# Layer 3's last FFN unit beside the attention's head, its second call in halves, and products of constants in layer 1

## The chip, the cores and the metric

The kernel runs on one core of a Trainium2 chip. A core has five engines with queues of their own: TensorE (PE) multiplies matrices into PSUM, VectorE (DVE), ScalarE (ACT) and GpSimd (POOL) work on what lies in SBUF or PSUM, and SyncE (SP) starts most transfers.[...] The metric is the device time of one launch in microseconds. The kernel before took 2889.82 us (median of three runs, 2889.73 to 2892.66).

## What is computed

Four sequences of 512 rows and 128 features pass through four layers. Each layer is a half-weighted FFN, an attention and the same FFN again:

```python
x = x + 0.5 * _L1_ffn_ref(_layernorm(x, axis=-1), ...)
x = x + _L1_attn_ref(_layernorm(x, axis=-1), ...)
x = x + 0.5 * _L1_ffn_ref(_layernorm(x, axis=-1), ...)
...
x = x + 0.5 * _L3_ffn_ref(_layernorm(x, axis=-1), ...)
x = x + _L3_attn_ref(_layernorm(x, axis=-1), ...)
x = x + 0.5 * _L3_ffn_ref(_layernorm(x, axis=-1), ...)
return x
```

Layer 1's "FFN" contains a causal attention of 16 heads of 8 features, followed by experts of which two are chosen per row. Layer 3's attention has the same heads without a mask. Layer 3's FFN is two transformer blocks with attention over windows of 64 rows; this is one block, without its attention:

```python
x = x + o @ wo
h = shift_token(x)
mu = h.mean(-1, keepdims=True)
var = h.var(-1, keepdims=True)
h = (h - mu) / jnp.sqrt(var + 1e-05) * lg + lb
h = h @ w1 + b1
a, g = jnp.split(h, 2, axis=-1)
h = a * jax.nn.gelu(g, approximate=False)
x = x + h @ w2 + b2
```

All values are float32. A float32 product appears in the trace as two instructions of PE.

## The kernel before

Everything stays in SBUF: x and its normed copy y with rows on partitions, yT with features on partitions. b counts the four sequences, S = 512 is the length of one, P = 128, TB = 4 tiles of 128 rows. The stages run in the order of the reference. Instructions marked "in order" (mm_in_order, L163, and the like) keep the program's order on their engine; the others are placed by a scheduler.

**Dense attention** (dense_attention, L735) serves layer 1's FFN, called twice (masked), and layer 3's attention (not masked). There are 16 units, one for each sequence b and each j of 0 to 3; a unit has four steps, a step two halves. A half of maxima (L751) multiplies queries and marked keys of two head groups, in products that use 32 rows of the array, into one of two "q" banks, and DVE takes the row maxima (L772 masked, L767 not). queries turns a unit's maxima (pm) and adds them to the queries (qx). scores multiplies again into the one "k" bank (pk), weights takes the exponential on ACT (L802), and with_values multiplies with the values into the one "o" bank (po). Maxima run LEAD = 5 steps ahead of scores, so the loop at L869 starts at step -5: these first ten halves of maxima, with what prepare does before them for b = 0 (normed features, queries, keys, values; its early steps are called at once, L863), are the **head**. In the last five steps, the **tail**, there are no maxima left. The PSUM banks are MIX: two banks as one "k" tile, two "q" tiles of two banks, one "o" and one "m". All other products share the single "m".

**Chains and ticks.** Work that isn't urgent is put into a chain: a list of small steps, each with a gap. tick (L259) is called after every half and runs the chain steps that are due, at most one with products. In this way a finished sequence is normed for the next stage (leave_normed: statistics, scaling, turn), and layer 1's experts are worked off. With routed set, in layer 1's second call, each sequence also gets its router logits.

**Layer 3's FFN** (l3_ffn, L1549) has eight units, one for each of two blocks and each b, with four steps each. project, to_features, weights, exponentials, turn_weights and with_values are the window attention, in a pipeline six steps deep. What follows in a unit is a list of parts (L1809), each with the step after which it comes: attended (pz, the output product, and the shifted copy h2), mean (pm), variance (pvar, and an inverse root in ten small steps on POOL, L1739), spread (dg), normed (pb), hidden three times (two products of 512 columns each, pag, then GELU and a multiplication, hh), close_unit (pz2) and leave (pt_z; adds to x, and in the first call norms it for the attention, in the second sends it out). For all but the last unit the parts lie among the next unit's steps. For the last unit, b = 3 of the second block, the loop at L1820 runs on for 14 steps with nothing beside the parts. Then l3_attn opens its own pools and begins with b = 0.

Of the kernel before, what the change touches and what calls it, by code (L numbers as in the profile page):

```python
# [28 lines left out]
P = 128  # L29
# [74 lines left out]
def tile_macaron(ctx, tc, x_in, const_in, vec_in, w0_in, ws_in, ws3_in, w2f_in, w3_in, out):  # L104
# [61 lines left out]
    def transpose_in_order(dst, src):  # L166
        tc.keep_in_program_order(transpose(dst, src))

# [566 lines left out]
    def dense_attention(sb, prepare, finish, wo, masked, tiles=None):  # L735
# [119 lines left out]
        for u, (b, j) in enumerate(units):  # L855
# [6 lines left out]
            if j == 0:  # L862
                for at, f in prepare(b, seq(b)["vh"], seq(b)):  # L863
                    if b or at >= -LEAD:
                        later.setdefault((n + math.floor(at), int(at % 1 * 2)), []).append(f)
                    else:
                        f()

        for n in range(-LEAD, n_steps + 5):  # L869
            for half in range(2):  # L870
                pk = scores(n, half) if 0 <= n < n_steps else None
                if n + LEAD < n_steps:
                    maxima(n + LEAD, 1 - half)
                if pk is not None:
                    weights(n, half, pk)
# [673 lines left out]
    def l3_ffn(w3, tag, first):  # L1549
        with pool(tag) as sb, banks(tag + "ps", d=3, m=2):  # L1550
# [8 lines left out]
            def tmp(name):  # L1559
                return sb.tile([P, S], F32, tag="tmp", name=name, bufs=4)  # L1560
# [7 lines left out]
            def pair(name):  # L1568
                return bank("d", name)

            def shift(dst, src):

                act_copy(dst[0:64], src[0:64])
                nc.gpsimd.memset(dst[64:128, 0:1], 0.0)
                nc.vector.tensor_copy(dst[64:128, 1:S], src[64:128, 0 : S - 1])
# [116 lines left out]
            def with_values(step):  # L1692
# [12 lines left out]
                if t == 0:  # L1705
                    u_state[u]["oT"] = sb.tile([P, 4, S], F32, tag="oT", name="oT")
# [3 lines left out]
            def attended(u):  # L1710
                l, b = units[u]
                oT = u_state[u]["oT"]
                pz = bank("m", "pz")
                for fc in range(4):
                    mm_in_order(pz, W(l, "wo").rearrange("p (c n) -> p c n", n=D)[:, fc, :], oT[:, fc, :], fc == 0, fc == 3)
                z = yT[:, b, :]
                nc.vector.tensor_add(z, pz, z)
                h2 = sb.tile([P, S], F32, tag="h2", name="h2", bufs=2)
                shift(h2, z)
                u_state[u]["h2"] = h2  # L1720

            def mean(u):
                h2 = u_state[u]["h2"]
                pm = bank("m", "pm")
                mm_in_order(pm, onesm, h2)
                nc.vector.tensor_sub(h2, h2, pm)
                sq = tmp("sq2")
                act(sq, h2, AF.Square)
                u_state[u]["sq"] = sq

            def variance(u):

                sq = u_state[u].pop("sq")
                pv = bank("m", "pvar")
                for t in range(TB):
                    mm_in_order(pv[:, 2 * t : 2 * t + 2], sq[:, ts(t, P)], onesm[:, 0:2])
                rs = sb.tile([P, TB], F32, tag="rs", name="rs", bufs=2)
                nc.vector.tensor_copy(rs, pv[:, : 2 * TB].rearrange("p (t i) -> p t i", i=2)[:, :, 0])
                inverse_root(sb, rs, rs, "ir4", ALU.add, 1e-5, nc.gpsimd)  # L1739
                u_state[u]["rs"] = rs  # L1740

            def spread(u):

                rs = u_state[u].pop("rs")
                dg = tmp("dg")
                nc.vector.scalar_tensor_tensor(
                    dg.rearrange("p (t n) -> p t n", n=P), rows(ident, TB), float(D), bcast(rs, P), ALU.mult, ALU.mult
                )
                u_state[u]["dg"] = dg

            def normed(u):
                l, b = units[u]
                h2 = u_state[u]["h2"]
                pb = bank("m", "pb3")
                mm_in_order(pb, onesm, u_state[u].pop("dg"))
                nc.vector.scalar_tensor_tensor(h2, h2, W(l, "lg"), pb, ALU.mult, ALU.mult)

            def hidden(u, c):
                l, b = units[u]
                at, n = HCH[c]  # L1760
                h2, w1 = u_state[u]["h2"], W(l, "w1")
                if c == 0:
                    u_state[u]["hh"] = sb.tile([P, 3, S], F32, tag="hh", name="hh")
                p = pair("pag")
                mm_in_order(p[:n, 0:512], w1[:, HID + at : HID + at + n], h2)
                mm_in_order(p[:n, 512:1024], w1[:, at : at + n], h2)
                ge = tmp("ge")
                act(ge[:n, :], p[:n, 0:512], AF.Gelu, bias=W(l, "b1g")[:n, c : c + 1])
                nc.vector.scalar_tensor_tensor(
                    u_state[u]["hh"][:n, c, :], p[:n, 512:1024], W(l, "b1a")[:n, c : c + 1], ge[:n, :], ALU.add, ALU.mult  # L1770
                )

            def close_unit(u):
                l, b = units[u]
                hh = u_state[u]["hh"]
                w2 = W(l, "w2").rearrange("p (c n) -> p c n", n=D)
                z = yT[:, b, :]
                pz = bank("m", "pz2")
                for c, (_, n) in enumerate(HCH):
                    mm_in_order(pz, w2[:n, c, :], hh[:n, c, :], c == 0, c == 2)  # L1780
                nc.vector.scalar_tensor_tensor(z, pz, W(l, "b2"), z, ALU.add, ALU.add)
                del u_state[u]

            def leave(b):
                pt = bank("m", "pt_z")
                for t in range(TB):
                    transpose_in_order(pt[:, ts(t, P)], yT[:, b, ts(t, P)])
                xb = x[:, ts(b, TB), :].rearrange("p t d -> p (t d)")
                nc.vector.scalar_tensor_tensor(xb, pt, 0.5, xb, ALU.mult, ALU.add)
# [218 lines left out]
```

## Time and profile before

| | before |
|---|---|
| median of the runs | 2889.82 us |
| profiled execution | 2886.26 us |
| span of its trace, first to last instruction | 2884.6 us |
| granted TensorE clock, mean | 0.871 |
| PE busy | 2245.8 us (78%) |
| DVE busy | 1788.8 us (62%) |
| ACT busy | 1243.1 us (43%) |
| POOL busy | 911.9 us (32%) |

A profile is one execution. The view in 40 slices gives each engine's busy share in tenths and, as PEclk, the clock that the throttle granted TensorE. A matmul takes longer at a lower clock and still counts as busy, so a busy PE with a low clock is a slow one. The timeline gives start, duration, engine, line, operation, and in brackets how long the engine had been idle and what ended that.

### The profile page before, as it was taken

The page shows a single profiled execution, that of the slowest core. Times are in us where ns is not written, and L with a number is a line of the kernel's source. Part 1 is how long each engine was busy: PE and PEld are TensorE (multiplying, and loading weights), DVE is VectorE, ACT ScalarE, POOL GpSimd, SP SyncE. Part 2 cuts the span into 40 slices and gives each one's busy share as a digit, 9 for nine tenths or more (in the row PEclk, how much of TensorE's full clock was granted, in tenths as well). Part 3 has the DMA queues.
Part 4 walks back from the last instruction along what each step waited for, and adds up shares of the span by engine and source line. Part 5 has one row for each costly group of instructions (what it writes and reads, how often), then busy time and mean ns, then how long its engine had stood idle before and what let it go on. Part 6 is the DMA issues. An engine that isn't in the chain of part 4 may idle for free. (4 is left out here: it accounts for less than half of the span.)

```text
span 2884.6 us, 46981 instructions
## 1 busy us (share of the span) xinstructions
PE 2245.8 (78%) x17562; PEld 1171.8 (41%) x17562; DVE 1788.8 (62%) x4844; ACT 1243.1 (43%) x2678; POOL 911.9 (32%) x1704
## 2 busy tenths in 40 slices
PE   4387448988678899758668578997789998789987
PEld 2154123333343333347458455555322222455553
DVE  4745576775675677544754577776356554777763
ACT  3154214433333433313423277776134444567763
POOL 1022012233121231213313486774100000777661
PEclk8578659999887999869868799999689999899998
DMA  3052010000000000027007210000000000110000
GB/s 135 11 158 67 0 59 1 1 1 1 1 1 1 1 1 5 4 75 257 9 16 272 72 25 19 22 21 8 0 1 1 1 1 1 26 23 21 22 20 12
DMA packets 33772, 99.14 MB, mean 34 GB/s; under 512 B 6184, under 2 KB 12072, under 8 KB 33032
## 3 DMA queue, kind: packets, MB, share of 16 engines
q1 hardware_dynamic: 30616, 88.03, 9.4%
q0 software_dynamic: 2496, 5.12, 0.8%
q8 instruction: 139, 2.28, 0.3%
q10 hardware_dynamic: 432, 2.98, 0.3%
q14 instruction: 89, 0.73, 0.1%
HBM read 66.88 MB, written 14.55 MB: 28 GB/s over the span
## 5 line engine op out<-in xcount | busy, mean ns | idle before, releaser
L802 ACT ACTIVATE PT<-pk_at 128x1024 f32<-128x1024 f32 (+3 forms) x384 | 310.8, 809 | 543.9 <-PE pq_at L164 470.6
L164 PE MATMUL pk_at<-qx,km 32*128 32x512 f32 (+3 forms) x1536 | 368.1, 556 | 61.3 <-ACT PT L802 56.3
L164 PE MATMUL po_at<-PT,vh 128*32 128x512 f32 (+3 forms) x1536 | 328.7, 510 | 4.4 <-POOL PT L805 4.2
L772 DVE CUSTOM_DVE_ANT_0 s<-pq_at,cst 128x384 f32<-128x384 f32 (+3 forms) x512 | 248.4, 485 | 97.2 <-PE pq_at L164 85.8
L1563 ACT ACTIVATE s<-s,nm,rn 128x128 f32<-128x128 f32 x512 | 245.5, 482 | 2.1 <-DVE nm L1669 1.9
L805 POOL TENSOR_SCALAR_AFFINE_SELECT PT<-PT 128x256 f32<-128x256 f32 x256 | 106.8, 419 | 411.5 <-ACT PT L802 411.4
L164 PE MATMUL pq_at<-km,qT 32*128 32x384 f32 (+3 forms) x1024 | 225.2, 528 | 13.7 <-DVE nm L772 7.3
L164 PEld LDWEIGHTS pk_at<-qx,km 32*128 32x128 f32 x1536 | 119.7, 189 | 266.2 <-ACT PT L802 206.7
L767 DVE TENSOR_REDUCE nm<-pq_at 128x2 f32<-128x1024 f32 x128 | 156.2, 1225 | 104.4 <-PE pq_at L164 103.9
L1618 POOL TENSOR_TENSOR t<-t,t 128x1024 f32<-128x1024 f32 x64 | 151.3, 2364 | 132.1 <-DVE t L1614 131.7
L161 PE MATMUL pt_y<-ident,y 128*128 128x128 f32 x224 | 55.1, 376 | 157.6 <-DVE y L214 118.4
L164 PE MATMUL p_qk<-w,hT 128*128 128x512 f32 x256 | 146.5, 701 | 11.0 <-DVE t L1614 9.1
L164 PE MATMUL pq_at<-km,t 32*128 32x512 f32 x512 | 149.4, 689 | 7.0 <-DVE nm L767 4.9
L164 PEld LDWEIGHTS po_at<-PT,vh 128*32 128x32 f32 x1536 | 55.7, 109 | 222.2 <-issue 144.0
L161 PE MATMUL pt<-ident,s 128*128 128x128 f32 x640 | 92.2, 291 | 62.8 <-POOL s L1681 36.7
L241 ACT COPY yT<-pt_y 128x512 f32<-128x512 f32 x56 | 32.7, 584 | 242.8 <-PE pt_y L161 242.7
L1681 POOL TENSOR_TENSOR s<-s,sm 128x1024 f32<-128x1024 f32 x64 | 121.4, 1897 | 49.3 <-DVE sm L1680 41.2
L1611 DVE TENSOR_TENSOR t<-p_qk,w 128x1024 f32<-128x1024 f32 x64 | 78.3, 1223 | 71.7 <-ACT sq L1563 71.4
L1563 ACT ACTIVATE sq<-p_qk 128x1024 f32<-128x1024 f32 x64 | 65.5, 1023 | 127.7 <-PE p_qk L164 76.0
L161 PEld LDWEIGHTS pt<-ident,s 128*128 128x128 f32 x640 | 77.5, 149 | 95.2 <-POOL s L1681 51.5
L161 PEld LDWEIGHTS pt_y<-ident,y 128*128 128x128 f32 x224 | 35.0, 173 | 188.3 <-issue 119.0
L1305 DVE SCALAR_TENSOR_TENSOR hT<-pa,w,sg 128x128 f32<-128x128 f32 x184 | 51.8, 344 | 84.8 <-ACT sg L1304 63.7
(428 smaller groups left out, 5145.3 us busy)
## 6 DMA issues: line engine op xcount, KB each, us to landing
w<-in_w2f_dram SPq DMA_DIRECT2D x46, 836.0 KB, 5.9
vb<-v SPq DMA_DIRECT2D x112, 128.0 KB, 2.2
skew<-qe SPq DMA_DIRECT2D x16, 512.0 KB, 3.0
rel<-skew SPq DMA_DIRECT2D x64, 128.0 KB, 3.3
w<-in_w_dram SPq DMA_DIRECT2D x1, 4147.0 KB, 12.4
w<-in_w_dram SPq DMA_DIRECT2D x1, 3200.0 KB
od<-o SPq DMA_DIRECT2D x46, 64.0 KB, 5.0
yd<-y SPq DMA_DIRECT2D x8, 256.0 KB, 2.3
```

The costliest lines, as they stand in the source:

```text
L161: return nc.tensor.transpose(dst, src, ident[: src.shape[0], : src.shape[0]])
L164: tc.keep_in_program_order(nc.tensor.matmul(dst, lhsT=lhsT, rhs=rhs, start=start, stop=stop))
L241: by_order(nc.scalar.copy(yT[:, b, :], pt))
L767: nc.vector.tensor_reduce(to, pq.rearrange("p (i n) -> p i n", i=2), AX.X, ALU.max)
L772: nc.vector.tensor_tensor_reduce(s[:, :nk], pq[:, i * 512 : i * 512 + nk], causal[:, S - nk :], 1.0, -BIG, ALU.add, ALU.max, nm[:, qt, at ...
L802: by_order(nc.scalar.activation(PT[:, :, q0:], pk[:, :, q0:], AF.Exp, scale=SC8))
L805: nc.gpsimd.affine_select(d, d, pattern=[[0, 2], [1, P]], base=0, channel_multiplier=-1, compare_op=ALU.is_ge, fill=0.0)
L1305: nc.vector.scalar_tensor_tensor(hT[s][:, c, :], pa[:, ts(c, P)], b1[:, c : c + 1], sg, ALU.add, ALU.mult)
L1563: tc.keep_in_program_order(nc.scalar.activation(*args, **kw))
L1611: nc.vector.tensor_mul(by_head(t1), by_head(p3), over(tab[:, 0]))
L1618: nc.gpsimd.tensor_add(t1, t1, t2)
L1681: nc.gpsimd.tensor_mul(s, s, bcast(sm, P))
```

## The change

Layer 1's dense attention gets products of two constants (onesm, a matrix of 1/128, and columns of the constants cst) into a PSUM bank that nobody reads: of 512 columns after each step of the head that prepare calls at once, of 256 in each half of the head's loop, and in the second call of 256 in each half of the tail. Layer 3's attention, which isn't masked, gets a tick in place of the first kind.

The last unit of layer 3's FFN leaves the list of parts. In the first call its steps become a chain, so that the ticks of the attention's head run them, one at a time, with the attention's PSUM banks; leave of the unit before stands among them. Its tiles come from a pool that outlives both stages. In the second call each step is done in two halves of 256 columns, and the unit before leaves after the first step. The last unit's inverse root is on DVE in both calls.

```diff
@@ -166,6 +166,10 @@
     def transpose_in_order(dst, src):
         tc.keep_in_program_order(transpose(dst, src))
 
+    def idle_product(tag, n):
+
+        mm_in_order(bank(tag, "idle")[:, :n], onesm, cst[:, :n])
+
     def bcast(ap, n):
 
         return ap[:, :, None].to_broadcast([ap.shape[0], ap.shape[1], n])
@@ -865,12 +869,20 @@
                         later.setdefault((n + math.floor(at), int(at % 1 * 2)), []).append(f)
                     else:
                         f()
+                        if masked:
+                            idle_product("o", S)
+                        else:
+                            tick()
 
         for n in range(-LEAD, n_steps + 5):
             for half in range(2):
                 pk = scores(n, half) if 0 <= n < n_steps else None
                 if n + LEAD < n_steps:
                     maxima(n + LEAD, 1 - half)
+                if masked and n < 0:
+                    idle_product("o", S // 2)
+                elif masked and routed and n_steps - LEAD <= n < n_steps:
+                    idle_product("q", S // 2)
                 if pk is not None:
                     weights(n, half, pk)
                 if 1 <= n <= n_steps:
...
-    def l3_ffn(w3, tag, first):
+    def l3_ffn(w3, tag, first, rb):
...
-                return bank("d", name)
...
+                return bank("d" if "d" in psum["bufs"] else "q", name)
+
+            def shift(dst, src, at=slice(0, S)):
+
+                act_copy(dst[0:64, at], src[0:64, at])
+                a = max(at.start, 1)
+                if at.start == 0:
+                    nc.gpsimd.memset(dst[64:128, 0:1], 0.0)
+                nc.vector.tensor_copy(dst[64:128, a : at.stop], src[64:128, a - 1 : at.stop - 1])
...
+            def attended(u, at=whole):
                 l, b = units[u]
                 oT = u_state[u]["oT"]
+                n = at.stop - at.start
                 pz = bank("m", "pz")
                 for fc in range(4):
-                    mm_in_order(pz, W(l, "wo").rearrange("p (c n) -> p c n", n=D)[:, fc, :], oT[:, fc, :], fc == 0, fc == 3)
+                    mm_in_order(
+                        pz[:, :n], W(l, "wo").rearrange("p (c n) -> p c n", n=D)[:, fc, :], oT[:, fc, at], fc == 0, fc == 3
+                    )
                 z = yT[:, b, :]
...
+                nc.vector.tensor_add(z[:, at], pz[:, :n], z[:, at])
+                if at.start == 0:
+                    u_state[u]["h2"] = rb.tile([P, S], F32, tag="h2", name="h2", bufs=2)
+                shift(u_state[u]["h2"], z, at)
...
+                eng = nc.vector if u == len(units) - 1 else nc.gpsimd
+                inverse_root(rb, rs[:, :n], rs[:, :n], f"ir{n}", ALU.add, 1e-5, eng)
...
+            def hidden(u, c, at=whole):
...
+                mm_in_order(p[:n, 0:m], w1[:, HID + a : HID + a + n], h2)
+                mm_in_order(p[:n, 512 : 512 + m], w1[:, a : a + n], h2)
...
+            def leave(b, at=whole):
                 pt = bank("m", "pt_z")
+                t0, n = at.start // P, (at.stop - at.start) // P
+                for t in range(n):
+                    transpose_in_order(pt[:, ts(t, P)], yT[:, b, ts(t0 + t, P)])
+                tiles = slice(b * TB + t0, b * TB + t0 + n)
...
-                    nc.sync.dma_start(out[:, ts(b, TB), :], x[:, ts(b, TB), :])
+                    nc.sync.dma_start(out[:, tiles, :], x[:, tiles, :])
...
-            later = {}
+            later, last = {}, len(units) - 1
             for u in range(len(units)):
-                for f, after, place in parts:
+                for f, after, place in parts[: -1 if u == last - 1 else None] if u < last else ():
                     later.setdefault((u * TB + after, place), []).append((f, u))
...
+            rest = [attended, mean, variance, spread, normed]
+            rest += [lambda u, at, c=c: hidden(u, c, at) for c in range(3)] + [close_unit, lambda u, at: leave(units[u][1], at)]
+            if first:
+                spare = chain(units[last][1])
+                for f in rest:
+                    spare(1, lambda f=f: f(last, whole), f is not spread)
+                    if f is variance:
+                        spare(1, lambda: leave(units[last - 1][1]))
+            else:
+                for f in rest:
+                    for at in (slice(0, S // 2), slice(S // 2, S)):
+                        f(last, at)
+                    if f is attended:
+                        leave(units[last - 1][1])
 
 
...
-    l3_ffn(w3, "l3f", True)
-    l3_attn()
-    l3_ffn(w3, "l3g", False)
+    with pool("l3r") as rb:
+        l3_ffn(w3, "l3f", True, rb)
+        l3_attn()
+        l3_ffn(w3, "l3g", False, rb)
```

mean, variance, spread, normed, hidden and close_unit take the same argument at as attended, and work on its columns. In the order of instructions that the change gives, layer 1's first call has two idle products ahead of its first turn, the second call three ahead of pw; the first of each waits for DVE's last reader of the bank. One scaling of layer 3's tables by vec stands behind the keys of the first head instead of ahead of them. In layer 3's attention PE's order is pz, p of the keys, pm, p, pvar, pt_z of b = 2, p of the queries, p, pb, and then products of maxima with the three pag pairs, pz2, pt_z and pt_y between them.

## The prediction

> **What bounds the kernel now.** I began with the page's 40 slices, because the change names three places, and looked for idle TensorE and for a low granted clock there.
>
> ```profile
> span 2884.6 us, 46981 instructions
> ...
> PE   4387448988678899758668578997789998789987
> ```
>
> That line must be read with the clock line of the same view; one slice is 72 us.
>
> ```profile
> PEclk8578659999887999869868799999689999899998
> ```
>
> The clock is half in the slice at 361 to 433 us (layer 1's first dense attention begins at 388; the other 5 is layer 0, not touched) and low again in those at 1154 and 2019 us. A slice hides shorter dips, so around the changed places I cut the trace into stretches of 4 or 5 us: busy microseconds and instructions of PE, weight loads, DVE, ACT, POOL, then the granted clock.
>
> ```profile
> 416.00:420.00 4.00, 3.62 (x15) 1.72 (x13) 3.00 (x14) 0.00 (x0) 0.00 (x0) 0.50 0.00 0
> 420.00:424.00 4.00, 3.95 (x17) 1.79 (x17) 1.99 (x10) 0.17 (x1) 0.00 (x0) 0.50 0.00 0
> 900.00:904.00 4.00, 2.71 (x12) 0.52 (x8) 1.49 (x5) 1.18 (x2) 0.41 (x1) 0.50 0.00 2
> 1190.00:1195.00 5.00, 5.00 (x14) 0.88 (x12) 0.00 (x0) 1.62 (x2) 0.57 (x2) 0.50 0.00 0
> 2098.00:2102.00 4.00, 4.00 (x12) 1.65 (x12) 2.96 (x3) 0.00 (x0) 0.00 (x0) 0.50 0.00 0
> 2118.00:2122.00 4.00, 3.81 (x21) 0.90 (x18) 2.43 (x2) 2.05 (x2) 0.00 (x0) 1.00 0.00 0
> ```
>
> TensorE is busy yet at half speed, so in these heads (and in the tail at 1190) it is the bound through its clock. The timeline gives the price of half speed for one shape, the four instructions of a half's score products:
>
> ```profile
> 1165.32 1.13 PE L164 MATMUL pk_at<-qx,km 32*128 32x512 f32 x4
> 1166.44 2.08 PE L164 MATMUL pq_at<-km,qT 32*128 32x512 f32 x4
> ```
>
> Layer 3 is bound otherwise, by chains in which one engine works and the rest wait. Last FFN unit of the first call, first product of the attention, its first exponential:
>
> ```profile
> 2033.72 3.70 PE L164 MATMUL pz<-oT,w 128*128 128x512 f32 x8 [0.21 <-DVE oT L1707]
> ...
> 2070.53 2.07 PE L164 MATMUL p<-yT,ws 128*128 128x512 f32 x2 [0.68 <-ACT yT L241]
> ...
> 2106.97 1.02 ACT L802 ACTIVATE PT<-pk_at 128x1024 f32<-128x1024 f32 x1
> ```
>
> So 36.8 us of FFN remainder and then 36.4 us of attention head, one after the other; only b=3 is in the first, only b=0 in the second. The end of the kernel is the same remainder:
>
> ```profile
> 2852.97 3.70 PE L164 MATMUL pz<-oT,w 128*128 128x512 f32 x8 [0.21 <-DVE oT L1707]
> ...
> 2864.84 0.69 DVE L1746 SCALAR_TENSOR_TENSOR dg<-ident,rs 128x512 f32<-128x512 f32 x1 [2.85 <-POOL rs L194]
> ...
> 2868.58 7.64 PE L164 MATMUL pag<-h,w 128*128 128x512 f32 x12 [0.92 <-DVE h L1756]
> ...
> 2880.50 0.69 DVE L1789 SCALAR_TENSOR_TENSOR x<-pt_z,x 128x512 f32<-128x512 f32 x1 [0.75 <-PE pt_z L161]
> ```
>
> 28.2 us from pz to the last x, and 3.4 us more to the end of the span.
>
> **Part 1, idle products.** Added: 12 products of 512 columns and 30 of 256, full 128 rows. Such a product of 512 takes 0.86 us at full clock (p_qk: four instructions in 1.72 us on the chain that ended last) and 2.08 us at half (pk at 402.39); of 256, half of each by length. They add 23 us of PE time at full clock, all in heads and one tail.
>
> Here a rule speaks against the part. The Trainium skill (TensorE: Matmul & The Clock Gate, Part 1) says that some 3.4 us of sustained matmuls release the throttle. By it a busy stream warms itself, the idle products only add work, and the part costs a few us. The rows above disagree: PE busy 5.00 of 5 us at 1190, and 4.00 of 4 at 2098, at clock 0.50. What these share is products of 32 rows, two at a time, half the array. Full-row streams do rise: the pag products from 2868.58 run at 1.04 us each and from about 2872.4 at 0.43, after 3.8 us. I go by the rows: full rows between the half-filled ones should raise the clock and hold it.
>
> First call. PE runs on from pt_y at 392.0, so I put the rise at about 396. The first two idle products wait for DVE's last reader of that bank (x<-pb, to 386.4); only pt_y at 392.0 is behind them. The one after pt_y delays pw by about 1 us; then pq and pk take 0.9 instead of 2.08, and km comes at 401.8 instead of 405.1. One scaling of w by vec (1.18 us, DVE) now stands behind km, where it was hidden before: maxima begin at 403.9 instead of 406.6, gain 2.6. From there to qx is 14.4 us now. DVE's own work in it is 9.9 us (4 x 0.74 at 512, 4 x 0.60, 4 x 0.47, 6 x 0.33, values 0.69); PE with an idle product needs 0.86+0.43 at 512, less than DVE's 1.48. So about 10.5: gain 3.9. The first two steps cost 3.2 and 2.65 instead of 2.3: gain 1.2. **7.5 us.**
>
> Second call. Three idle products stand ahead of pw, after the linear attention's last reader (874.3): pw 2.6 us later. pq and pk at full clock give back most; km is 0.4 later. The maxima to qx take 10.5 instead of 14.0 (883.8 to 897.8), and the steps from 898.5 to 911.2, 12.7 us at half clock, take 8.3 by the pace at full clock (2.3 each at 512, from 918.2 to 920.5; 1.85 each at 384, from 427.6 to 431.2). 3.5+4.4-0.4 = **7.5 us**.
>
> Tail. From 1186.2 to 1201.8 ten halves alternate pk and po at half clock. At full clock with an idle product they take some 11 us (PE-bound: 0.65+0.43+0.86 at 384). Of 4.5 I keep **3 us**, since DVE's expert sums follow at 1202.5 and the gate's chain on DVE ends only at 1188.4.
>
> These operations were not in the trace; the bounds for the three together are 24 us gained and, if all stay at half clock, 44 lost (below).
>
> **Part 2, the remainder beside the head.** Nothing is removed but b=3's place: its steps go one per tick between those of attention b=0. They share the attention's single "m" bank, so each product waits for the reader of the one before. I walked PE's and DVE's new order with the rows' durations (1.13 a product with its latency, 0.7 a DVE pass of 512, POOL's add 1.26, maxima 1.23). pz 2033.7 to 2037.4; yT 38.1; p(k), pm, p(ks), pvar, pt_z of b=2, p(q), p(qs), pb, each some 1.9 us apart with its reader: pb ends at 2053.5. The inverse root is on DVE (8 x 0.2), interleaved. Ahead of the first maxima DVE has h and the four scalings of b=2 (1.1), so these begin at 55.8. Then ten halves of maxima with three pag pairs, pz, pt_z and pt_y between them, DVE-bound at about 2 us: qx at 75.5, exponential at 77.2. Against 2106.97 that is 29.8. But around 2043 to 2050 PE does little but pvar and transposes, and before, the clock fell about 1 us after just such a pvar (it ends at 2861.8; the row of 2860 to 2864 shows 0.86, so 2.9 us of it at 1.00). If it falls, three products and the first pag lose some 6 us before it rises. I take **24 us**; bounds 14 (all at half clock: six products +0.95, three pag +1.9, ten halves with little cover) and 30. Behind the moved steps: b=3's statistics and scalings (2.7 us of DVE) now lie among maxima, hidden by PE's pace of 2.3 a half, else +1. POOL's four memsets (2.4 us) and the bias adds to x wait for nobody on the path; POOL loses ten root steps. SP gets nothing here.
>
> **Part 3, the end in halves.** pz0 ends at 54.8, pz1 at 56.7; while one half is on PE the other is on DVE or ACT. A DVE pass of 256 costs 0.42 against 0.69 (maxima at 256), so split passes cost DVE 0.15 each. x of b=2 now stands before h of the second half (0.7). sub 59.5, sq 60.0, pvar 60.6, both roots on DVE to 62.1 and 63.2 (POOL took 62.07 to 64.80 for one), pb, first h at 64.0 where it was 68.5: gain 4.5. pag: 12 x 0.43 = 5.2 at full clock, 7.5 if it has fallen as before (7.64). From its end to x 3.8 instead of 5.0, for hh, pz2, yT, pt_z and x are each half as long. Gain 5.9 with a fallen clock, 8.1 without. **6.5 us.** SP issues two output transfers of half size; only the second counts, and the 3.4 us stay.
>
> **Sum.** 7.5+7.5+3+24+6.5 = 48.5 us. The profiled execution took 2886.26 us (span 2884.6 and 1.7 around it), which gives 2837.8; the median of the runs shown is 3.6 above it: **2841**.
>
> **Rivals.**
> - *The idle products raise the clock but don't hold it*; part 1 is worth nothing net: -30.5, 2859. For it: the second head reached 0.76 in the row of 888 to 892 and fell to 0.50. Against it: no full-row product stood between the maxima there.
> - *Layer 3's head stays cold*: 14 instead of 24, and the end at 5: 2851. For it: at 2070 to 2082 PE was busy two thirds with full-row products at 0.50. Against: it starts from full clock this time.
> - *Slower*: idle products don't count for the clock. Place: the two heads and the tail. At half clock each of 256 costs 1.04 on a bound PE: 30 x 1.04 = 31; those of 512 put 4 us into the first chain and 9 into the second: 44 in all. It decides once that passes the 30 which layer 3 gives: 2904. Only the pag row speaks against it, and strongly.
> - *The change doesn't do what it says*: layer 3's one bank keeps the two chains in series. The new order shows p(k) directly behind pz, so I give it little.
>
> **How the numbers follow.** Forecast 0.60 (own range 2828 to 2852), no hold 0.17, cold head 0.15, slower 0.05, in series 0.03 (about no change). The lower end 2824 takes the upper bounds of all parts (24+30+8), the upper end 2866 covers both milder rivals together in part. A measurement of this kernel can tell about 0.2% (5.8 us) from no change: faster 0.92, same 0.03, slower 0.05.
>
> **What would show it.** Clock 1.0 from about 396 to 430 and from 874 to 915; first exponential of layer 3's attention some 43 us after pz; first h of the last unit 11 us after pz. Wrong if the rows at 400 to 424 keep 0.50, if the maxima of layer 3 wait for pag's bank more than for DVE, or if another stage changes by more than 5 us.

## The result and the profile after

| | us |
|---|---|
| before, median of 4 runs (lowest to highest) | 2891.24 (2889.73 to 2894.17) |
| changed, median of 4 runs (lowest to highest) | 2860.84 (2856.48 to 2867.22) |
| ratio, 95% interval | 0.9895 (0.9873 to 0.9917) |
| profiled execution before / changed | 2886.26 / 2856.48 |
| changed again, on another chip: median, ratio | 2855.85, 0.9871 (0.9853 to 0.9889) |

The change saves 30 to 37 us of 2890; the forecast was 48.5. From the view in 40 slices (now 71 us each) the two lines that were shown of before, TensorE's busy tenths and its granted clock:

```profile
span 2854.8 us, 47242 instructions
...
PE   4377468988678898859566678998799999688988
...
PEclk8588769999889998959777789999899999899998
```

The clock's digit went from 5 to 6 in the slice that begins at 357 us (first head), from 7 to 9 at 856 (second head), from 8 to 9 at 1142 (tail) and from 6 to 8 at 1998 (layer 3's head). But behind the tail, at 1213, it went from 6 to 5. The same cut into short stretches as before (busy microseconds and instructions of PE, weight loads, DVE, ACT, POOL, then the granted clock):

```profile
392.00:396.00 4.00, 4.00 (x6) 1.30 (x4) 4.00 (x11) 0.20 (x1) 2.09 (x2) 0.50 0.00 0
396.00:400.00 4.00, 3.84 (x8) 1.35 (x8) 3.51 (x11) 0.77 (x2) 0.00 (x0) 0.94 0.00 0
...
416.00:420.00 4.00, 2.40 (x20) 0.73 (x12) 2.35 (x7) 2.52 (x3) 1.62 (x2) 1.00 0.00 0
420.00:424.00 4.00, 3.96 (x20) 1.02 (x20) 1.58 (x6) 0.81 (x1) 0.81 (x2) 0.57 0.00 0
900.00:904.00 4.00, 2.81 (x20) 0.77 (x20) 2.51 (x9) 1.76 (x3) 0.81 (x2) 1.00 0.01 2
1190.00:1195.00 5.00, 5.00 (x28) 2.11 (x28) 0.55 (x2) 1.56 (x3) 0.81 (x2) 1.00 0.00 0
...
2098.00:2102.00 4.00, 3.68 (x24) 0.91 (x24) 1.89 (x3) 1.42 (x3) 0.00 (x0) 1.00 0.00 0
```

All the stretches that stood at 0.50 now show 1.00, except 420 to 424: the idle products do raise the clock, where the forecast put the rise (396), and hold it until they stop. Layer 3's head and the end of the kernel, from the timeline:

```profile
2038.71 3.67 PE L164 MATMUL pz<-oT,w 128*128 128x512 f32 x8 [0.89 <-DVE oT L1725]
...
2052.36 2.08 PE L164 MATMUL p<-yT,ws 128*128 128x512 f32 x2 [1.19 <-DVE x L1815]
...
2089.62 1.02 ACT L806 ACTIVATE PT<-pk_at 128x1024 f32<-128x1024 f32 x1 [5.73 <-PE pq_at L164]
...
2829.16 3.72 PE L164 MATMUL pz<-oT,w 128*128 128x256 f32 x16
2829.28 0.69 DVE L1725 COPY oT<-po 128x512 f32<-128x512 f32 x1 [0.34 <-PE po L164]
...
2839.74 0.48 DVE L1779 SCALAR_TENSOR_TENSOR h<-h,w,pb 128x256 f32<-128x256 f32 x1 [0.54 <-PE pb L164]
2840.33 7.13 PE L164 MATMUL pag<-h,w 128*128 128x256 f32 x24
...
2851.11 0.42 DVE L1815 SCALAR_TENSOR_TENSOR x<-pt_z,x 128x256 f32<-128x256 f32 x1 [0.20 <-PE pt_z L161]
```

From pz to the first exponential it is 50.9 us where it was 73.3, and from pz to the end of the last x 22.4 where it was 28.2. At the end, pz itself starts earlier: its first half does not need DVE's last copy of oT, behind which the whole pz of before stood:

```profile
2852.22 0.69 DVE L1707 COPY oT<-po 128x512 f32<-128x512 f32 x1 [0.34 <-PE po L164]
```

From the start of that copy, which both kernels have, to the end of the last x it is 22.3 us where it was 29.0, so the end gains 6.7 and not 5.8. In layer 3's head, pz stands at 2038.71, 5 us later than before: by then everything that layer 1 gained is gone. That calls for a table by place. The **lag** is how much later the same ACT instruction starts than in the profile of before (a negative lag is earlier), at the places named by before's time; the last column is the difference of the spans. The runs other than the first are those of the next section.

| profile | ahead of first head (385) | behind (436) | ahead of second head (860) | behind (915) | layer 1 done (1262) | layer 3's head (2030) | behind it (2120) | span |
|---|---|---|---|---|---|---|---|---|
| changed | -1.7 | -5.9 | -1.9 | -5.1 | +0.9 | +4.9 | -18.9 | -29.8 |
| changed, again | +1.3 | -4.6 | +1.5 | -1.8 | +4.2 | +4.9 | -18.9 | -29.9 |
| in series (same code to 2030) | -1.2 | -7.1 | -4.3 | -7.6 | -1.8 | -2.0 | -1.4 | -10.7 |
| idle products alone | +0.7 | -3.6 | +0.6 | -2.6 | +3.9 | +5.9 | +4.0 | +4.0 |
| no idle products | -2.5 | -2.6 | +0.7 | +0.7 | +0.7 | 0.0 | -19.6 | -26.1 |
| idle products in layer 3's head only | -2.5 | -2.6 | +0.7 | +0.7 | +10.1 | +12.7 | -16.6 | -24.0 |

In each of the first four the first head gains 4.3 to 5.9 us and the second 3.2, and in each the stretch between the heads takes 2.8 to 6.1 back. But the last two have the code of before up to 2030, and they differ by 12.7 us there. So what lies between the heads can't be laid to the change from one profile; that is what the experiments are for.

### The profile page after: what moved, and what is told of

Same layout as the page of the kernel before. It is cut to its first block, busy times and chain, and to the rows that moved or that the text cites. A ratio compares the mean times of both kernels' runs of the same rounds, so it can differ in the third digit from the quotient of the medians.

```text
span 2854.8 us, 47242 instructions
## 1 busy us (share of the span) xinstructions
PE 2246.9 (79%) x17676; PEld 1178.8 (41%) x17676; DVE 1793.1 (63%) x4879; ACT 1244.2 (44%) x2683; POOL 908.0 (32%) x1684
## 5 line engine op out<-in xcount | busy, mean ns | idle before, releaser
L164 PE MATMUL pq_at<-km,qT 32*128 32x128 f32 (+3 forms) x1024 | 217.9, 502 | 9.7 <-DVE nm L776 5.0
L164 PE MATMUL p_qk<-w,hT 128*128 128x512 f32 x256 | 140.0, 674 | 11.0 <-DVE t L1632 9.2
```

Source lines behind the costliest of these rows:

```text
L164: tc.keep_in_program_order(nc.tensor.matmul(dst, lhsT=lhsT, rhs=rhs, start=start, stop=stop))
```

## The experiments

Times are medians; beside each stands its ratio to the kernel before, run on the same chip, with the 95% interval. Differences to the changed kernel are by these ratios, from its first measurement (0.9895); by its second (0.9871) each would be 7 us larger. The edits are to the changed kernel, if nothing else is said.

**No idle products.** Layer 3's two parts alone.

```diff
-                        if masked:
-                            idle_product("o", S)
-                        else:
+                        if not masked:
                             tick()
...
-                if masked and n < 0:
-                    idle_product("o", S // 2)
-                elif masked and routed and n_steps - LEAD <= n < n_steps:
-                    idle_product("q", S // 2)
```

> The changed kernel without any of the 42 idle products: only layer 3's two parts are left. Theory (the idle products raise the clock in the heads, but layer 1 and layer 2 give the gain back in other dips, so that they bring nothing net): 2858 to 2865 us, as the changed kernel's 2861, and a clock of 0.50 again around 400 to 424. Rival 1 (they bring the 18 us of the forecast and layer 3 brings less than walked): about 2879. Rival 2 (they cost time net, as the lag of layer 1 and 2 in the one profile says: 2.5 to 6 us): 2854 to 2858.

2857.0 us, 0.9891 (0.9874 to 0.9907): the changed kernel's ratio without any of its idle products. Rival 1 falls, 18 us are not there. Rival 2, that the products cost time, had 2854 to 2858 and is not decided by this run; the next one decides it.

**Idle products alone**, added to the kernel before (the edit's base is that kernel).

```diff
                     else:
                         f()
+                        if masked:
+                            idle_product("o", S)
...
                     maxima(n + LEAD, 1 - half)
+                if masked and n < 0:
+                    idle_product("o", S // 2)
+                elif masked and routed and n_steps - LEAD <= n < n_steps:
+                    idle_product("q", S // 2)
```

> The kernel before with the 42 idle products of layer 1 and nothing else. Theory (they gain 4 to 6 us in the first head and 3 in the second and lose as much in layer 1's later dips and behind the tail): within 4 us of the kernel before, 2885 to 2893. Rival (their 18 us are real and the runs without them in the changed kernel had luck): 2871. Where the heads are, the lag must fall by 4 to 6 and by 3 all the same.

2889.9 us over 14 runs, 0.9991 (0.9979 to 1.0004): -2.6 us, between -6 and +1. Both heads show their gain in the lag (-4.3 and -3.2), as expected, and the time does not. This is the measure of part 1: neither its 18 us nor a cost of 2.5 to 6.

**Idle products on 32 rows.**

```diff
-        mm_in_order(bank(tag, "idle")[:, :n], onesm, cst[:, :n])
+        mm_in_order(bank(tag, "idle")[:, :n], onesm[:32], cst[:32, :n])
```

> The changed kernel with the idle products on 32 of the 128 rows; they take the same time on PE. Theory (what raises the clock is the filled array, not a busy PE): the rows at 400 to 424 and 893 to 910 stay at 0.50, and each idle product is then pure cost at half clock: 2861 plus 10 to 40 us. Rival (any product between the half-filled ones counts, since it closes gaps): the same time and clock as the changed kernel, 2861.

2889.2 us over 14 runs, 1.0004 (0.9992 to 1.0016): some 32 us slower than the changed kernel, and as much slower than the kernel without any idle products (2857.0 on the same chip). All of layer 3's gain is used up. Stretches of its first head:

```profile
404.00:408.00 4.00, 4.00 (x19) 2.51 (x18) 2.94 (x11) 2.50 (x3) 0.00 (x0) 0.50 0.02 4
408.00:412.00 4.00, 4.00 (x20) 2.63 (x18) 2.09 (x5) 0.00 (x0) 0.00 (x0) 0.50 0.00 0
```

PE is busy in every microsecond and the clock stays at 0.50; in the changed kernel the same products with 128 rows give 1.00 there. What counts for the clock is not busy time alone, but how much of the array the products fill. Rows are one side of it, columns may be the other: in the stretch of before at 1190, busy for 5.00 of 5 us at 0.50, half of PE's work has 128 rows, but 32 columns:

```profile
1190.35 1.92 PE L164 MATMUL po_at<-PT,vh 128*32 128x512 f32 x4
```

(No run has such products alone.) Here the rule of the Trainium skill (TensorE: Matmul & The Clock Gate, Part 1: some 3.4 us of sustained matmuls release the throttle) is too wide, as the rows of before had said.

**Shorter idle products in the heads.**

```diff
                 if masked and n < 0:
-                    idle_product("o", S // 2)
+                    idle_product("o", S // 2 if order[(n + LEAD) % TB] == TB - 1 else P)
```

> The changed kernel with idle products of 128 columns instead of 256 in the heads' maxima wherever those are of fewer than 512 columns. Theory (an idle product of 256 columns takes PE 0.63 us, not the 0.43 of the forecast, so that PE and not DVE sets the pace of the maxima at 1.48 us a half): the first head's maxima to qx take 10.7 instead of 12.0 us and the second head's 11.9 instead of 13.3; the whole by as much, 2858, if nothing gives it back. Rival (DVE sets the pace, or 128 columns do not hold the clock): 12 us and more to qx, 2861 to 2866.

2868.3 us (2857.7 to 2879.0), 0.9905 (0.9881 to 0.9929). First head, PE's products at full clock, and then stretches of the first and of the second head:

```profile
402.85 0.49 PE L164 MATMUL idle<-cst,onesm 128*128 128x128 f32 x2
403.26 0.49 PE L164 MATMUL pq_at<-km,qT 32*128 32x128 f32 x4
403.68 0.49 PE L164 MATMUL idle<-cst,onesm 128*128 128x128 f32 x2
```

```profile
408.00:412.00 4.00, 4.00 (x12) 1.82 (x10) 1.49 (x4) 0.00 (x0) 0.00 (x0) 0.50 0.00 0
...
886.00:890.00 4.00, 3.51 (x8) 1.06 (x6) 3.19 (x12) 0.00 (x0) 0.00 (x0) 1.00 0.00 0
```

In the second head the clock held and the lag fell by 1.0 us between 860 and 895, where the changed kernel's rose by 0.3: 1.3 of the 1.4 that were expected. In the first it fell at 405.0 and stayed down to 428.9, so maxima to qx took 19.1 us instead of 12.0. Half right: PE does set the pace, but products of 128 columns are no safe hold on the clock.

**Without the tail's idle products.**

```diff
-                elif masked and routed and n_steps - LEAD <= n < n_steps:
-                    idle_product("q", S // 2)
```

> The changed kernel without the idle products in the tail of layer 1's second dense attention (those in the two heads stay). Theory (the tail's products only move the cold stretch from 1187 to 1197 to the experts behind it, 1216 to 1246): 2858 to 2863 us; the cold stretch after 1216 is short again (some 20 us in two pieces, as before). Rival (they keep the 3 us of the forecast): 2864.

2858.2 us, 0.9899 (0.9885 to 0.9913), no difference from the changed kernel that can be measured. The cold stretch behind the tail is 1221.7 to 1238.8 and 1242.2 to 1249.0, 24 us in two pieces, instead of 1215.8 to 1246.5 in one. But the tail itself was cold from 1184.2 to 1208.1 in this profile and cost 6.4 us there, so the profile is no proof that the products cost anything. In the changed kernel's own the tail gains 0.4 us up to 1205 and the experts behind it lose 3.1.

**A delay behind the first head's first query tile**, to move the work against the clock's windows.

```diff
             nc.vector.tensor_add(qx, pm, seqs[b]["q"])
+            if masked and not routed and u == 0:
+                for _ in range(2):
+                    nc.vector.tensor_add(qx, pm, seqs[b]["q"])
```

> The changed kernel with two DVE passes more (2 x 0.69 us) behind the first query tile of layer 1's first dense attention, so that all that follows stands 1.4 us later against the clock's windows. Theory (the dip at 516 to 523 comes from the phase alone: in the profiles with it, those of the changed kernel and of the one without the tail's products, the work stands at -0.6 us, modulo 3.41, against the windows as the kernel before has them, and in three without it at 0, +0.5 and +0.8): no dip there, and the 2.6 us that the changed kernel lost between 436 and 560 are not lost: lag -4.5 at both. Rival (the dip belongs to the faster head): dip and loss stay, lag -4.5 at 436 and -1.9 at 560. The time of the whole, 2861, can move by 5 either way.

2867.2 us, 0.9921 (0.9900 to 0.9941). The lag was -4.1 at 436 and -1.7 at 560, and the dip was there, 517.3 to 524.2. As an experiment it failed: the windows stood 1.3 us later in this execution, so that the work came to -0.16 and not to +0.8. What answers the question is other profiles of the same code. Every cold stretch in these profiles lasts a multiple of 3.41 us, and the Trainium skill (TensorE: Matmul & The Clock Gate, Part 1) says that the clock is judged in free-running windows of 3413 ns. Take the work's lag at 500 less the shift of the windows, modulo 3.41, and call it the phase. The dip at this change of unit is there at -0.59, -0.57, -0.56, -0.26 and -0.16 (five profiles) and not at 0 to +0.85 (eight, four of which have all of layer 1's idle products). The lag by itself does not part them: with the dip it is -6.8, -6.0, -5.9, -4.1 and +2.9, without it -7.1 to +5.1. Two of these profiles, the changed kernel first and then the one in series:

```profile
512.00:516.00 4.00, 2.23 (x24) 1.09 (x22) 3.56 (x7) 2.45 (x5) 3.45 (x4) 0.99 0.00 0
516.00:520.00 4.00, 3.60 (x17) 1.14 (x19) 2.00 (x8) 1.02 (x1) 0.41 (x1) 0.50 0.01 2
```

```profile
512.00:516.00 4.00, 2.39 (x24) 1.04 (x24) 3.37 (x12) 1.44 (x4) 2.30 (x4) 1.00 0.00 0
516.00:520.00 4.00, 3.28 (x32) 1.74 (x28) 3.12 (x9) 2.42 (x3) 0.81 (x2) 1.00 0.01 2
```

At a change of unit PE does little for some 4 us, in both alike, and yet the clock goes down in one alone. That fits a clock that falls only where such a stretch lies inside one window; no run set the phase on purpose, so it is a fit to thirteen profiles. But three executions came to one phase by themselves, -0.59 to -0.56 (the changed kernel, the one without the tail's products, and the one with layer 3's head filled too), and they show the same nineteen cold stretches, of the same lengths, from 420 to 1168; the changed kernel again, at +0.78, shows a different series up to 760. The rival, that the dip belongs to the faster head, is out: the one in series has the faster head and no dip, and its lag is -7.1 at 436 and at 560.

**One idle product more at each change of unit**, to keep those dips away.

```diff
             nm = nms[j % 2]
+            if masked and qt == 0 and half == 0 and step > LEAD:
+                mm_in_order(pq[:, P:S], onesm, cst[:, P:S])
```

(It stands ahead of the line of nm.)

> The changed kernel with one idle product more at each change of unit in layer 1's dense attentions (27 of 384 columns and 128 rows, into the unused part of the maxima's bank, ahead of a hole of 0.6 to 0.8 us that PE has there in the traces). Theory (what the heads gain is given back by clock dips that a change of unit starts, when its thin products fall inside one of the clock's 3.41 us windows): no dips between 424 and 720 and between 920 and 1175, the lag of layer 1's heads is kept, 2861 - 5 to 12 = 2849 to 2856 us. Rival 1 (the give-back is some other limit, which the heads only reach earlier): the dips go, the time stays at 2861. Rival 2 (the fill delays the maxima of a DVE-bound place): up to 27 x 0.4 = 11 us slower, 2872.

2878.8 us, 0.9959 (0.9944 to 0.9975), 18 us slower. Most changes of unit have no hole for it. One of them, the product and what comes after it:

```profile
448.39 0.91 PE L164 MATMUL pq_at<-cst,onesm 128*128 128x384 f32 x2
449.23 0.63 PE L164 MATMUL po_at<-PT,vh 128*32 128x256 f32 x4
449.79 0.70 PE L164 MATMUL pk_at<-qx,km 32*128 32x512 f32 x2
```

The po product waits 0.84 us behind the fill, and what follows starts 0.8 later than in the changed kernel again. The trace has 28 of these products (not 27). Where the clock is alike on both sides, each costs between 0.18 us (at 517, where PE did have a hole, of 0.6) and 0.85; by the mean of some 0.6 that is 17 us. The dip at 516 is gone, but not those at 608, 693, and 710 to 734. Rival 2 was right in kind, with 11 us put for what cost 18.

**In series**: the first call's last unit finished ahead of layer 3's attention.

```diff
-                spare = chain(units[last][1])
                 for f in rest:
-                    spare(1, lambda f=f: f(last, whole), f is not spread)
+                    f(last, whole)
                     if f is variance:
-                        spare(1, lambda: leave(units[last - 1][1]))
+                        leave(units[last - 1][1])
+                finish_chains()
```

> The changed kernel with the first call's last unit finished before layer 3's attention begins, as in the kernel before. Theory (the two chains side by side bring what the lag of the profiles shows, 17 to 23 us): 2861 + 20 = 2881 us, first exponential about 67 us after pz. Rival (the overlap is worth no more than the 14 of the lower bound, the rest of layer 3's gain lies in the root on DVE and in the end): 2875.

2884.4 us over 19 runs, 0.9980 (0.9968 to 0.9992): 25 us above the changed kernel, so the overlap is worth that and not 14. From pz to the first exponential 73.1 us, as before: the 6 us that I had expected of the root on DVE do not show in this profile.

**The end in one piece.**

```diff
-                    for at in (slice(0, S // 2), slice(S // 2, S)):
-                        f(last, at)
+                    f(last, whole)
```

> The changed kernel with the last unit's end in one piece of 512 columns instead of two of 256; its inverse root stays on DVE. Theory (the halves bring what the lag of the one profile shows, 5.6 us, of which some 1.5 come from the root on DVE): 2861 + 4 = 2865 us; from pz to the last x 26 to 27 us. Rival (the end's gain is all from the root on DVE): 2861. The kernel is the changed one up to the end, so that its profile also shows whether layers 1 and 2 lag as in the first profile.

2862.7 us, 0.9915 (0.9902 to 0.9928). Its end in the timeline:

```profile
2829.12 3.70 PE L164 MATMUL pz<-oT,w 128*128 128x512 f32 x8 [0.79 <-DVE oT L1725]
...
2834.74 1.10 PE L164 MATMUL pm<-h,onesm 128*128 128x512 f32 x2 [1.49 <-DVE h L1593]
2837.34 1.87 PE L164 MATMUL pvar<-onesm,sq 128*128 128x2 f32 x8 [1.50 <-ACT sq L1579]
...
2856.95 0.69 DVE L1815 SCALAR_TENSOR_TENSOR x<-pt_z,x 128x512 f32<-128x512 f32 x1 [0.75 <-PE pt_z L161]
```

From pz to the end of the last x 28.5 us, no better than the 28.2 of before, and not the 26 to 27 I had expected: the root on DVE is taken up by leave, which now stands ahead of h (pm starts 5.6 us after pz, before 5.1), and by pvar at half clock. From DVE's last copy of oT it is 29.3 us, where before has 29.0 and the changed kernel 22.3. So the halves bring all of the end's gain: 7 us here, 5.8 by the ratios.

**Idle products in layer 3's head instead of layer 1's.** The chain there leaves PE holes of 0.8 to 1.0 us, and 0.50 from 2052 to 2066 in the changed kernel.

```diff
-                        if masked:
-                            idle_product("o", S)
-                        else:
+                        if not masked:
+                            idle_product("o", S // 2)
                             tick()
+                            idle_product("o", S // 2)
...
-                if masked and n < 0:
+                if not masked and n == -1:
                     idle_product("o", S // 2)
-                elif masked and routed and n_steps - LEAD <= n < n_steps:
-                    idle_product("q", S // 2)
```

> The changed kernel without layer 1's idle products, and with idle products of 256 columns in layer 3's head instead: two at each step of preparation, two before the first step. Theory (that head is a chain with holes of 0.8 to 1.0 us on PE and at 0.50 from 2040 to 2068; filled, it stays at full clock: seven products of 1.13 instead of 2.08 us, two pairs of pag of 1.95 instead of 3.6, and the dip at 2085 goes): 6 to 10 us from the 2857 of the kernel without idle products, 2847 to 2851. Rival (an idle product stands in the chain's way by 0.6 us a time, as in the heads of layer 1): 2857 to 2862.

2860.3 us (2852.3 to 2867.0), 0.9881 (0.9859 to 0.9904). The time is the rival's, but the head did what the theory expected: pz, its first p, its first exponential,

```profile
2046.98 3.60 PE L164 MATMUL pz<-oT,w 128*128 128x512 f32 x8
2050.41 0.59 PE L164 MATMUL idle<-cst,onesm 128*128 128x256 f32 x2
2051.36 1.13 PE L164 MATMUL p<-yT,ws 128*128 128x512 f32 x2 [0.35 <-DVE yT L1739]
...
2092.79 1.02 ACT L806 ACTIVATE PT<-pk_at 128x1024 f32<-128x1024 f32 x1 [4.79 <-PE pq_at L164]
```

45.8 us, 5.1 less than the changed kernel's and 9.3 less than without any idle products, and no cold stretch from 2037 to 2436. The hole ahead of p holds the idle product and PE still waits 0.35 us for DVE, so it costs nothing there; the one ahead of pz (2046.47) delays it by 0.5. But the profile lost 12.7 us in layers 1 and 2, with the very code of the kernel without idle products. The two part at 1125; first that kernel, then this:

```profile
1125.00:1129.00 4.00, 3.81 (x22) 1.28 (x20) 3.21 (x11) 1.34 (x3) 0.41 (x1) 1.00 0.00 0
...
1200.00:1205.00 5.00, 5.00 (x38) 2.39 (x36) 0.69 (x1) 1.53 (x4) 1.22 (x3) 1.00 0.00 0
```

```profile
1125.00:1129.00 4.00, 3.81 (x10) 1.12 (x8) 2.10 (x7) 1.03 (x2) 0.41 (x1) 0.64 0.00 0
...
1200.00:1205.00 5.00, 5.00 (x18) 1.23 (x16) 0.00 (x0) 1.77 (x3) 0.82 (x2) 0.50 0.01 3
```

Up to 1125 their lags agree to 0.1 us; then, at phases of 0.00 and 0.07, one dip comes in the one and not in the other, and others follow it.

**Both**: the changed kernel with the idle products of layer 3's head as well, and **the changed kernel again** beside it.

> The changed kernel with the idle products in layer 3's head as well (as in the run that has them alone). Theory (that head's gain, 5.5 us more than the changed kernel's by the lags, is a place of its own and stays): 5 us below the changed kernel run beside it, about 2855, with no cold stretch between 2040 and 2110. Rival (the gain is lost in the spread of what follows, as layer 1's): the same as the changed kernel within 3 us.

> The changed kernel once more, on the same chip as the run beside it. Theory (outside layer 3's two places its gain over the kernel before is within what the clock's dips spread): ratio to the kernel before 0.9885 to 0.9905, layer 3's head again 21 us faster, the lag at its start anywhere between -2 and +9. Rival (the first measurement was unlucky and layer 1's products bring several us): 0.985 or less.

2852.4 us (2848.9 to 2856.0), 0.9858 (0.9839 to 0.9876), and 2855.9 us (2852.8 to 2857.1), 0.9871 (0.9853 to 0.9889). From pz to the first exponential the first takes 45.8 us again, and no stretch from 2024 to 2195 is cold. It is 3.4 us below the changed kernel, in the direction expected, but the intervals overlap; of all kernels here it has the lowest median. The changed kernel's second ratio lies below the range I had expected and above the rival's.

## Why the prediction was right, and which of its steps failed

The time fell into the range and the direction was right, but 2841 was 20 us too low (of the forecast's 48.5 us the second measurement saves 37), and nearly all of it is one term. The forecast's own range, 2828 to 2852, was missed: the time lies in the wide range because that was drawn to take in the milder rivals, so that even a part 1 of nothing (2859) falls into it. That much is luck.

**Part 2, 24 us: right, with errors in it that cancel.** 22.4 us from pz to the first exponential in the profile, 25 in the runs (18.2 in the profile without idle products, where the clock stayed at 0.50 from 2041 to 2068). The clock fell behind the stretch of pvar, as the step had it: the p at 2052.36 takes 2.08 us. The 43 us named as a sign were the walk at full clock; with the fall it has 49, and 50.9 were measured. But the maxima were not DVE-bound at 2 us a half. In the changed kernel's profile:

```profile
2060.21 2.08 PE L164 MATMUL pq_at<-km,t 32*128 32x512 f32 x4
2062.21 3.65 PE L164 MATMUL pag<-h,w 128*128 128x512 f32 x4
2065.79 1.13 PE L164 MATMUL pq_at<-km,t 32*128 32x512 f32 x4
2066.62 0.75 DVE L1792 SCALAR_TENSOR_TENSOR hh<-pag,w,ge 128x512 f32<-128x512 f32 x1 [3.06 <-ACT ge L1579]
2067.42 1.98 PE L164 MATMUL pag<-h,w 128*128 128x512 f32 x4 [0.51 <-DVE hh L1792]
```

PE runs almost without a gap and DVE waits for it. From the first maxima to qx it takes 24.4 us where the walk has 19.7 and, for the fallen clock, some 3 more; that the maxima begin 23.6 us after pz, where it has 22.1 and 3 more, makes up for it. The bound of 30 was what the full clock would give; with idle products there it is 27.5 (73.3 to 45.8).

**Part 3, 6.5 us: right.** 5.8 us from pz, where 5.9 was the figure for a fallen clock, and it had fallen: the 24 passes of pag take 7.13 us. The first h ends 11.1 us after pz (forecast 11). What the sum did not have is that pz starts 0.9 earlier; with it the end gains 6.7.

**Part 1, 18 us: failed.** It brings 2.6 us (6 to -1). The mechanism was right: full rows raise the clock and hold it, 32 rows do not. Three things in the sum were not.

- *"PE with an idle product needs 0.86+0.43 at 512, less than DVE's 1.48"*, and with it *"of 256, half of each by length"*. Here is a piece of the changed kernel's first head:

```profile
405.85 1.13 PE L164 MATMUL pq_at<-km,qT 32*128 32x512 f32 x4
406.90 0.70 PE L164 MATMUL idle<-cst,onesm 128*128 128x256 f32 x2
407.53 0.91 PE L164 MATMUL pq_at<-km,qT 32*128 32x384 f32 x4
408.38 0.70 PE L164 MATMUL idle<-cst,onesm 128*128 128x256 f32 x2
409.00 0.91 PE L164 MATMUL pq_at<-km,qT 32*128 32x384 f32 x4
409.85 0.70 PE L164 MATMUL idle<-cst,onesm 128*128 128x256 f32 x2
```

  From the idle product's start to the next it is 0.62 us, not 0.43, and the four instructions at 512 take 1.05, not 0.86. A half of 512 costs PE 1.68 us where DVE needs 1.48, and one of 384 1.47 where DVE needs 1.20 (two passes at 0.60 each): PE sets the pace. "Half by length" does hold in a stream of products with all rows: pag's passes of 256 columns follow each other at 0.215 us from 2844 to 2847, which is 0.43 for two. Among the products of 32 rows it does not; no run isolates why. First head: maxima to qx 12.0 us instead of 10.5, and 1.2 lost in the dip at 420, behind the last idle product: 4.3 instead of 7.5 (5.9 in the profiles without that dip). Second head: maxima to qx 13.3 instead of 10.5; only the steps behind qx gained what was forecast (4.2, forecast 4.4).
- *"pq and pk at full clock give back most; km is 0.4 later"*. km starts at 882.43, 0.1 us later than before, but the work ahead of it had come 1.9 earlier: 2.0 lost. Together the second head gives 3.2 instead of 7.5, and the heads 7.5 to 9 instead of 15. The tail's 3 are 0.4, with 3.1 lost behind it in this profile.
- *That a head's gain reaches the end.* The sum carried it there as it was. In the runs 7.5 to 9 us in the heads become 2.6. From the start of the first head to layer 3's the six profiles with all the idle products and no other edit ahead of layer 3 need 6.6, 3.7, -0.8, 5.2, 3.2 and 3.6 us more than before, and the three without them, that of before among them, 0, 2.5 and 15.1. The mean is 2.3 lower with the products, which agrees with the runs, but each set spreads over more than that. One thing shows in all fourteen profiles, that of before among them: ahead of the first head (393) the work stands within 0.5 us of one phase, and ahead of the second (860.6) within 0.3, though the lags there go from -4.3 to +11.5. So from the one place to the other a profile differs from that of before by whole windows of 3.41 us, to within 0.4: by 0 in six of the seven with layer 1's idle products as in the changed kernel and by -1 in the seventh, by 0, +1 and +1 in the three without them. The first head's 4.3 to 5.9 us thus reach the second head in whole windows or not at all. Why 5 us of the heads' gain are lost on the average stays open: no experiment here held the phase fixed.

**The rivals.** "Raise the clock but don't hold it" gave 2859, nearest to the result, by the wrong mechanism: they hold it, from 396 to 420 and from 867.5 to 1072.3. "Layer 3's head stays cold" is out by 50.9 us. The slower rival's place and mechanism are real where the products have 32 rows, at 32 us instead of the 44 I had worked out. "In series" is out.

**Sums and readings.** Some slips, none of which decided anything: the first call's terms add up to 7.7, not 7.5; "Layer 3's head stays cold" comes to 2853 and not 2851, and the lower end to 2828: 2824 is reckoned from the profiled execution, the forecast from the median; and the pag products in the profile of before reached full clock at 2873.1, 4.5 us after their start, not at 2872.4.

**What would show it wrong** named another stage changing by more than 5 us. Layer 2, which isn't touched, came near it with 4.0 between 1262 and 2030 (-4.9 to +5.3 over all the profiles), layer 3's second FFN call with 4.6 up to its end, and in the profile with idle products in layer 3's head alone the untouched part of layer 1 behind 860 changed by 9.4: a threshold of 5 is below what one profile of this kernel can tell.

## What to carry to other kernels

A clock raised in one place is not a gain until the whole program's runs show it: measure such a part by itself, added to the kernel before, since one profile can differ by 12 us from another of the same code. Price a filler by its measured start-to-start time in its own shape, and put it into a hole of a chain that waits on another engine (layer 3's head) rather than into a stream that already keeps PE busy (the maxima, most changes of unit). Of the three parts the one that put two latency chains side by side brought most of the gain, and it could be walked to 2 us from the rows of the trace, though with two errors that cancelled.

## What the runs showed of the hardware

- Between other products, a product of 128, 256 or 512 columns with all 128 rows takes 0.41, 0.62 or 0.86 us of PE from start to start at full clock: there half the columns is not half the time. In the stream of pag 256 columns take 0.43.
- A PE that is busy without a gap with products of 32 rows stays at 0.50 (404 to 408 in the run with idle products on 32 rows); one product of 256 columns and 128 rows per half, 0.62 of 1.47 us, holds 1.00. With 128 columns, 0.41 us, it held in one head and fell in the other.
- Every cold stretch lasts whole windows of 3.41 us. Work at the same phase to these windows has the same cold stretches (nineteen of nineteen in three profiles), and layer 1's time from the first head to the second changes by whole windows.
- Two executions of the same instructions agree to 0.1 us in their lags up to 1125, and are 12.7 us apart at 2030; what the trace shows to differ between them is clock dips of 3.4 to 20 us. The time of one kernel spreads by 4 to 21 us over its runs, and a part that is worth 3 us needed some 14 runs a side to be bounded to 4.
